# A two-layer kernel: convolution in half-length passes of 256 channels, and nine rows in the middle sample products

## The chip, the cores and the metric

The kernel runs on one core of a Trainium2 chip. The metric is device time in microseconds (us); lower is better. All arithmetic is fp32. The engines are TensorE (PE, matmuls, with its weight loads shown as PEld), VectorE (DVE), ScalarE (ACT), GpSimd (POOL) and SyncE (SP); SP, ACT and POOL also issue DMAs.

## What is computed

The input x has 32 images of 128 channels and 32 x 32 pixels (L = 1024). Layer 0 is a group norm, an encoder to 1024 channels, a causal convolution of 64 taps for each channel, a GELU, a gated linear unit, a layer norm and a decoder. Layer 1 is a group norm and a deformable convolution of 8 x 8 taps for each channel, whose sampling offsets are a depthwise 3 x 3 convolution of its input. Both are added to their inputs. Cut to what matters:

```python
# layer 0, on u = group_norm(x), (B, 128, L)
h = jnp.einsum('bdl,de->ble', u, W_enc) + b_enc
K = 2.0 * jnp.einsum('dn,dnl->dl', Cc * Bd, vand).real      # 64 taps a channel
z = jnp.swapaxes(h, 1, 2)
y = irfft(rfft(z, n=L + 64) * rfft(K, n=L + 64), n=L + 64)[..., :L] + D[:, None] * z
y = gelu(swapaxes(y, 1, 2))
g = y @ W_glu + b_glu
g = g[..., :1024] * sigmoid(g[..., 1024:])
out = layernorm(h + g) @ W_dec + b_dec
# layer 1, on v = group_norm(x1): for each of 64 taps
px = gx[None] + koff_t[0] + off_t[..., 0]
py = gy[None] + koff_t[1] + off_t[..., 1]
ix, iy = px * sx - 0.5, py * sy - 0.5                        # sx = sy = 32/31
acc = acc + bilinear(v, iy, ix) * w_t[None, :, None, None]   # four gathers, 0 outside
```

## The kernel before

`tile_two_layer_kernel` runs four parts in turn. `ssm_kernel_table` works out the 64 taps of each channel and writes them to DRAM as `kp_d`, a row of 320 for each channel, reversed and padded with zeros. `ssm_convolution` makes y, the convolved and GELUed channels, in DRAM as `y_d`. `main_block` does the rest of layer 0 and layer 1. `deformable_redo` compares the largest offset of every image with `BOUND_X` and `BOUND_Y` and, for images beyond it, runs a general gather path; otherwise it does nothing more.

**The convolution stage** is written in a fixed order (`manual_schedule`): for each of eight blocks of 128 channels, `encode` and then `convolve`. In `encode` every image is eight matmuls, each with 128 positions of u as weights and 128 columns of `W_enc` moving; four fill one PSUM tile, which VectorE adds the bias to and writes into the tile z (line 227). z is 128 positions on the partitions, and for each channel four position blocks of 32 images; two such tiles of 64 KB a partition hold the two halves of the length. In the first block `encode` also computes the group norm of every image and stores it as `u_d`; the other seven load u again, 512 KB an image, five buffers ahead (line 236).

`convolve` goes over the block in groups of eight channels (`CG`). The convolution of one 128-position block is a matmul (line 299) with z as weights and a Toeplitz tile moving: for each channel 128 partitions x 192 columns, where partition p holds the row of `kp_d` shifted by p. Two triangles of it are zeros, and they are loaded with the rest (line 281, 768 KB a group, three buffers). Of the 192 result columns 128 belong to the block itself and 64 run over into the next one. ScalarE copies these to SBUF (line 307), VectorE adds them to the next block's partitions in PSUM (line 311; `ORDER` places the blocks so that a 64- and a 32-partition add do it, and one more takes the overlap from the first half of the length to the second), and ScalarE then writes the GELU into `yo` (line 320). The GELU of one tile is emitted after the next tile's copies and adds. A group of eight channels is stored by eight DMAs that POOL issues (line 332), four for each of two `yo` tiles out of six buffers. PSUM has two tiles for the encode and three for the convolution.

**The main block** interleaves two streams by an estimate of their cost (`run_along`): `first_part` of image b + 2, 292 matmuls of 512 columns (gate products at line 757, value products at line 780, encoder and decoder at lines 796 and 685), and `second_part` of image b, the sample products. The first two images' `first_part` and the last two images' `second_part` have no partner of that kind.

A sample product turns bilinear sampling into matmuls (line 1091). The image, transposed, is the weights: windows of 8 columns by 16 rows of pixels, so 128 on the partitions. Moving is `ds`, the product of two hat functions (line 1048), with one column for each slot (pairs of tap column and output column, 8 to 16 of them together), tap row ky and output row. The 17 packs of slots sum to 256; ky comes in four pieces of two; and the 32 output rows are cut in three by `rows_of(piece)`, for the windows that begin at rows 0, 8 and 16. Before, the middle cut has eight rows and begins at 15, 13, 11 and 9. A moving operand is therefore made of short runs of consecutive elements, one run of that many rows for each slot and ky. VectorE multiplies the result with the tap weights (line 1094), and GpSimd adds the two ky (line 1111) and accumulates (line 1116). How far an offset may go before a sample leaves its window is `BOUND_Y`. An fp32 matmul appears in the trace as two passes, each a weight load and a matmul record.

Of the kernel before, what the change touches and what calls it, by code (L numbers as in the profile page):

```python
# [7 lines left out]
F32 = mybir.dt.float32  # L8
AF = mybir.ActivationFunctionType
# [3 lines left out]
DRAM = bass.MemoryType.DRAM  # L13

P = 128
B, C, H, W = 32, 128, 32, 32
L = H * W
D = 1024
KD = D // P
# [6 lines left out]
TW = 192  # L26

KP0 = TW - 1
KPW = 320
CG = 8  # L30
# [152 lines left out]
def ssm_convolution(nc, tc, const, ins, x, u_d, kp_d, y_d):  # L183
# [5 lines left out]

    ORDER = (0, 2, 1, 3)
    NB = NJ // 2
    RW = TW - P
    QC = 4
    with tc.tile_pool(name="cvt", bufs=3) as tp, tc.tile_pool(
        name="cvz", bufs=1
    ) as zp, tc.tile_pool(name="cv1", bufs=1) as one, tc.tile_pool(
        name="cvu", bufs=5
    ) as up, tc.tile_pool(name="cvy", bufs=6) as yp, tc.tile_pool(  # L200
        name="cvg", bufs=4
    ) as gp, tc.tile_pool(
        name="cv_psz", bufs=2, space=PSUM
    ) as psz, tc.tile_pool(name="cv_psy", bufs=3, space=PSUM) as psy:
        w_enc = one.tile([P, D], F32, tag="w_enc", name="w_enc")
        nc.sync.dma_start(w_enc, ins["W_enc"])
        b_enc = one.tile([P, D], F32, tag="b_enc", name="b_enc")
        nc.sync.dma_start(b_enc, ins["b_enc_row"].to_broadcast([P, D]))

        def encode(k):  # L210

            z = [
                pool.tile([P, P, NB, B], F32, tag=f"z{g}", name=f"z_{k}_{g}")
                for g, pool in enumerate((one, zp))
            ]
            bias = b_enc[:, k * P : (k + 1) * P]

            def image(b, u):
                for g in range(2):
                    ps = psz.tile([P, NB, P], F32, tag="ps", name=f"psz_{k}_{b}_{g}")  # L220
                    for j in range(NB):
                        lo = (NB * g + ORDER[j]) * P
                        nc.tensor.matmul(  # L223
                            ps[:, j, :], u[:, lo : lo + P], w_enc[:, k * P : (k + 1) * P],
                            start=True, stop=True,
                        )
                    nc.vector.tensor_add(  # L227
                        z[g][:, :, :, b].rearrange("p d j -> p j d"),
                        ps,
                        bias[:, None, :].to_broadcast([P, NB, P]),  # L230
                    )

            if k > 0:
                for b in range(B):
                    u = up.tile([P, L], F32, tag="u", name=f"u_{k}_{b}")
                    nc.sync.dma_start(u, u_d[b])
                    image(b, u)
                return z

# [7 lines left out]
            for t in range(B + 3):  # L247
# [4 lines left out]
                if t < B:  # L252
                    u = up.tile([P, L], F32, tag="u", name=f"u_{k}_{t}")
# [10 lines left out]
                step(t)  # L264
            return z

        def convolve(k, z):
            rows = [t.rearrange("p d j b -> p d (j b)") for t in z]
            waiting = []

            def finish():
                for work in waiting:
                    work()
                waiting.clear()

            for g in range(P // CG):
                d0 = k * P + g * CG
                toe = tp.tile([P, CG, TW], F32, tag="toe", name=f"toe_{d0}")
                table = kp_d[d0 : d0 + CG, 0:TW]

                nc.sync.dma_start(
                    toe,
                    bass.AP(
                        tensor=table.tensor,
                        offset=table.offset,
                        ap=[[1, P], [KPW, CG], [1, TW]],
                    ),
                )
                yo = [
                    yp.tile([P, CG, P], F32, tag="yo", name=f"yo_{d0}_{i}") for i in range(2)  # L290
                ]
                for q in range(CG // QC):
                    c0 = q * QC
                    last = None
                    for i in range(2):
                        ps = psy.tile([P, 2, 512], F32, tag="ps", name=f"psy_{d0}_{q}_{i}")
                        ps = ps[:, :, : 2 * TW].rearrange("p h (c n) -> p h c n", c=2)
                        for c in range(QC):
                            nc.tensor.matmul(  # L299
                                ps[:, c // 2, c % 2, :],  # L300
                                rows[i][:, g * CG + c0 + c, :],
                                toe[:, c0 + c, :],
                                start=True,
                                stop=True,
                            )
                        over = tp.tile([P, 2, 2, RW], F32, tag=f"t{i}", name=f"t_{d0}_{q}_{i}")
                        nc.scalar.copy(over, ps[:, :, :, :RW])  # L307

                        def carry(to, rows, src):
                            own = ps[to : to + rows, :, :, P:TW]  # L310
                            nc.vector.tensor_add(own, own, src)  # L311

                        carry(64, 64, over[0:64])
                        carry(32, 32, over[64:96])
                        if i > 0:
                            carry(0, 32, last[96:P])
                        finish()

                        def gelu(to=yo[i][:, c0 : c0 + QC, :], ps=ps):
                            nc.scalar.activation(  # L320
                                to.rearrange("p (h c) l -> p h c l", c=2),
                                ps[:, :, :, RW:TW][:, :, :, ::-1],
                                AF.Gelu_apprx_tanh,
                            )

                        waiting.append(gelu)
                        last = over

                def store(yo=yo, d0=d0):
                    for i in range(2):  # L330
                        for j in range(NB):
                            nc.gpsimd.dma_start(  # L332
                                y_d[d0 : d0 + CG, :, i * NB + ORDER[j], :].rearrange(
                                    "d b l -> b d l"
                                ),
                                yo[i][j * B : (j + 1) * B],
                            )

                waiting.append(store)
            finish()  # L340


        with tc.manual_schedule():
            for k in range(KD):
                convolve(k, encode(k))


def deformable_general(nc, tc, const, ins, x1_d, out, image):
# [139 lines left out]
KY2 = 2  # L488
# [10 lines left out]
    (24, (30, 31)), (24, (32, 33)), (24, (34, 35, 36, 37)),  # L499
)  # L500
YWINDOWS = (0, 8, 16)
BOUND_X, BOUND_Y = 2.45, 3.25
HSUB = NCOL // P


# [5 lines left out]

def rows_of(piece):

    a, b = 15 - KY2 * piece, 23 - KY2 * piece
    return (0, a), (a, b - a), (b, H - b)


def weight_slots():
# [27 lines left out]
def main_block(nc, tc, const, ins, x, u_d, y_d, x1_d, out, offmax):  # L546
# [21 lines left out]
    with ctx:  # L568
# [562 lines left out]
        def measure(columns):  # L1131
# [3 lines left out]
        SECOND = sum(  # L1135
            measure(slots_of(n) * KY2 * ny)
            for n in range(NP) for i in range(PIECES) for _, ny in rows_of(i)
        )

# [178 lines left out]
```

## Time and profile before

| what | us |
|---|---|
| median of three runs | 13584.75 (13580.38 to 13586.92) |
| the profiled execution | 13588.92 |
| its span, first to last instruction | 13587.2 |
| of it, before the last matmul of line 299 ends | 1448 |
| sample products (L1091), busy, 13056 records | 4701.1 |
| gate and value products (L757, L780), busy, 8192 records each | 3986.4 and 3975.7 |
| convolution matmuls (L299), busy, 4096 records | 704.7 |
| encode matmuls (L223), busy, 4096 records | 568.6 |
| bias adds of the encode (L227), busy, 512 records | 516.2 |
| issues of y stores on POOL (L332), busy, 1024 records | 590.1 |

Busy times of one engine may overlap each other in time: matmuls are pipelined and their ends are modelled, so the pace of a matmul is read from start to start. A share of the whole span says little here, since the convolution stage (the first tenth) and the main block (the rest) have different limits.

### The profile page before, as it was taken

The numbers are of one execution on the slowest core, as the hardware profiler recorded it, in microseconds if no ns is written. First come the engines' busy times: TensorE is split into PE (matmuls) and PEld (weight loads), VectorE is DVE, ScalarE is ACT, GpSimd is POOL, SyncE is SP. The second block draws the span as 40 slices with busy tenths as digits, with TensorE's granted clock in tenths as the row PEclk, the third lists the DMA queues.
The fourth block names the chain that finished last, engine by engine and source line by source line (L and its number), as shares of the span: only waits on it lengthen the run. The fifth ranks groups of instructions, "written<-read, shape, count | busy, mean of one in ns | idle before, by whom it ended". The sixth has DMA issues, their size and how long they took to land.

```text
span 13587.2 us, 133930 instructions
## 1 busy us (share of the span) xinstructions
PE 13106.8 (96%) x40482; PEld 7248.5 (53%) x40482; DVE 8781.8 (65%) x12685; ACT 3291.8 (24%) x4767; POOL 9080.3 (67%) x8868
## 2 busy tenths in 40 slices
PE   7999899999999999999999999999999999999975
PEld 7888545555555555555555555555555555555533
DVE  7787226666666666666666666666666666666677
ACT  4333222222211122222222211112222222221145
POOL 2444227777777777777777777777777777777778
PEclk9999999999999999999999999999999999999988
DMA  7888428888888888888889888888888888988876
GB/s 244 275 277 273 132 90 231 234 239 236 231 227 231 233 235 238 238 236 232 230 234 239 235 229 229 231 232 237 238 237 236 232 230 235 240 235 231 230 198 175
DMA packets 1715626, 3105.77 MB, mean 229 GB/s; under 512 B 308306, under 2 KB 1018322, under 8 KB 1713874
## 3 DMA queue, kind: packets, MB, share of 16 engines
q1 hardware_dynamic: 1502290, 2641.91, 73.2%
q10 hardware_dynamic: 163456, 320.92, 6.6%
q0 software_dynamic: 49152, 134.28, 2.9%
q8 instruction: 329, 5.39, 0.2%
q14 instruction: 399, 3.27, 0.1%
HBM read 2630.36 MB, written 466.06 MB: 228 GB/s over the span
## 4 chain that ended last, share of the span: by engine, by line
PE 81%; DMA 9%; DVE 4%; ACT 2%; POOL 2%; issue 1%; SPq 1%; ACTq 0%; DVEq 0%; POOLq 0%
PE gpv L780 24%; PE gpg L757 23%; PE dps L1091 23%; DMA ds<-dhat 4%; PE gph L796 3%; PE gpo L685 3%; PE psy L299 3%; PE psz L223 2%; DMA y_d<-yo 2%; DMA dhat<-dh 2%; DVE z L227 1%; DVE ds L1048 1%; DMA dhy<-dhat 1%; POOL y_d L332 1%; ACT ds L1040 0%
## 5 line engine op out<-in xcount | busy, mean ns | idle before, releaser
L1094 DVE TENSOR_TENSOR dp<-dps,k_weight_slots 128x256 f32<-128x256 f32 (+17 forms) x6528 | 3087.1, 483 | 3109.5 <-PE dps L1091 2914.8
L1091 PE MATMUL dps<-ds,dxw 128*128 128x256 f32 (+18 forms) x13056 | 4701.1, 447 | 223.5 <-DVE ds L1048 177.5
L1116 POOL TENSOR_TENSOR dacc<-dacc,dp 128x256 f32<-128x256 f32 (+3 forms) x4736 | 4417.4, 933 | 396.5 <-DVE dp L1111 26.6
L1091 PEld LDWEIGHTS dps<-ds,dxw 128*128 128x128 f32 x13056 | 2472.7, 192 | 3203.6 <-issue 2537.5
L757 PE MATMUL gpg<-gy,g_w_glu 128*128 128x512 f32 x8192 | 3986.4, 593 | 23.5 <-DMA gy<-y_d 15.7
L780 PE MATMUL gpv<-gy,g_w_glu 128*128 128x512 f32 x8192 | 3975.7, 592 | 0.0
L1111 POOL TENSOR_TENSOR dp<-dp 128x448 f32<-128x448 f32 (+2 forms) x2142 | 2675.1, 1249 | 1882.1 <-DVE dp L1094 1879.4
L1048 DVE TENSOR_TENSOR ds<-ds,dhy 128x1024 f32<-128x1024 f32 (+3 forms) x2176 | 3148.6, 1447 | 762.4 <-DMA ds<-dhat 647.9
L757 PEld LDWEIGHTS gpg<-gy,g_w_glu 128*128 128x128 f32 x8192 | 1546.9, 190 | 1235.8 <-issue 964.9
L780 PEld LDWEIGHTS gpv<-gy,g_w_glu 128*128 128x128 f32 x8192 | 1551.7, 190 | 1155.3 <-issue 913.8
L818 POOL TENSOR_TENSOR gs<-gs,gq 128x512 f32<-128x512 f32 x448 | 628.5, 1403 | 1341.3 <-ACT gq L817 1341.3
L817 ACT ACTIVATE gq<-gr 128x512 f32<-128x512 f32 x448 | 282.3, 630 | 4673.6 <-DVE gr L809 4611.2
L332 POOL DMA_DIRECT2D y_d<-yo x1024 | 590.1, 583 | 869.7 <-ACT yo L320 699.2
L764 ACT ACTIVATE gs<-gpg,k_b_glu 128x512 f32<-128x512 f32 x512 | 351.8, 687 | 2488.0 <-PE gpg L757 2377.6
L953 ACT ACTIVATE dh<-dr,k_minus 128x624 f32<-128x624 f32 x768 | 621.7, 809 | 642.5 <-DMA dhat<-dh 563.1
L299 PE MATMUL psy<-toe,z 128*128 128x192 f32 x4096 | 704.7, 333 | 45.2 <-ACT yo L320 43.8
L299 PEld LDWEIGHTS psy<-toe,z 128*128 128x128 f32 x4096 | 667.5, 192 | 81.6 <-ACT yo L320 74.5
L311 DVE TENSOR_TENSOR psy<-psy,t 32x256 f32<-32x256 f32 (+1 forms) x1280 | 553.7, 433 | 204.7 <-ACT t L307 162.6
L788 DVE SCALAR_TENSOR_TENSOR gs<-gpv,k_b_glu,gs 128x512 f32<-128x512 f32 x512 | 379.7, 742 | 437.3 <-PE gpv L780 437.2
L687 POOL TENSOR_TENSOR gs<-gs,gr 128x512 f32<-128x512 f32 x448 | 634.7, 1417 | 0.0
L954 ACT ACTIVATE dh<-dh,one 128x624 f32<-128x624 f32 x768 | 626.3, 815 | 25.0
L223 PE MATMUL psz<-w_enc,u 128*128 128x128 f32 x4096 | 568.6, 293 | 44.9 <-DVE z L227 32.3
(162 smaller groups left out, 6052.4 us busy)
## 6 DMA issues: line engine op xcount, KB each, us to landing
dhy<-dhat SPq DMA_DIRECT2D x1536, 512.0 KB
ds<-dhat SPq DMA_DIRECT2D x1440, 512.0 KB
dhat<-dh ACTq DMA_DIRECT2D x768, 312.0 KB
y_d<-yo POOLq DMA_DIRECT2D x1024, 128.0 KB, 5.4
gy<-y_d SPq DMA_DIRECT2D x512, 256.0 KB
u<-u_d SPq DMA_DIRECT2D x224, 512.0 KB
toe<-kp_d SPq DMA_DIRECT2D x128, 768.0 KB
dxw<-dvt_d SPq DMA_DIRECT2D x1248, 64.0 KB
```

Source lines behind the costliest of these rows:

```text
L223: nc.tensor.matmul(ps[:, j, :], u[:, lo : lo + P], w_enc[:, k * P : (k + 1) * P], start=True, stop=True,)
L299: nc.tensor.matmul(ps[:, c // 2, c % 2, :], rows[i][:, g * CG + c0 + c, :], toe[:, c0 + c, :], start=True, stop=True,)
L332: nc.gpsimd.dma_start(y_d[d0 : d0 + CG, :, i * NB + ORDER[j], :].rearrange("d b l -> b d l"), yo[i][j * B : (j + 1) * B],)
L687: nc.gpsimd.tensor_add(sums[0], sums[0], r)
L757: nc.tensor.matmul(gate, w_glu[:, k, D + m * P : D + m * P + P], ys[k], start=(k == 0), stop=(k == KD - 1),)
L780: nc.tensor.matmul(val, w_glu[:, k, m * P : m * P + P], ys[k], start=(k == 0), stop=(k == KD - 1),)
L818: nc.gpsimd.tensor_add(sums[1], sums[1], sq)
L1048: nc.vector.tensor_mul(s[:, :m], s[:, :m], hy[:, :m])
L1091: nc.tensor.matmul(ps, xw[:, j, :], s[:, :m, :, y0 : y0 + ny], start=True, stop=True)
L1094: nc.vector.tensor_mul(prod[:, :m, :, y0 : y0 + ny], ps, w[:, :, :, None].to_broadcast([P, m, KY2, ny]),)
L1111: adder.tensor_add(prod[:, :m, 0], prod[:, :m, 0], prod[:, :m, 1])
L1116: nc.gpsimd.tensor_add(to, to, prod[:, slot : slot + nj, 0])
```

## The change

It has two parts that do not touch each other.

In the convolution stage, a pass is now 256 channels (`ZC`) of half the length, so four blocks of channels times two halves. z is one tile of the same 128 KB a partition. An image is four encode matmuls of 256 moving columns instead of eight of 128, u is loaded by halves (256 KB), and except in the first pass every fourth PSUM tile is evacuated by a ScalarE copy and a GpSimd add of the bias in place of the VectorE add. The Toeplitz tiles become three fixed tiles that are zeroed once; for every group of every half two DMAs, one for each 64 partitions, load only the band of 128 columns that is not always zero. The overlap from the first half of the length to the second goes through DRAM (`edges`): POOL stores it for each group in the first half, SP loads it in the second. `yo` has five buffers instead of six, one tile a group.

In the main block the middle cut of `rows_of` has nine rows instead of eight, beginning at 14, 12, 10 and 9, the last cut has one row less or the first has, and `BOUND_Y` goes from 3.25 to 2.25.

```diff
     ORDER = (0, 2, 1, 3)
+    ZC = 256
+    NTOE = 3
...
-    ) as up, tc.tile_pool(name="cvy", bufs=6) as yp, tc.tile_pool(
+    ) as up, tc.tile_pool(name="cvy", bufs=5) as yp, tc.tile_pool(
...
+        toes = []
+        for i in range(NTOE):
+            toe = one.tile([P, CG, TW], F32, tag=f"toe{i}", name=f"toe{i}")
+            nc.gpsimd.memset(toe, 0.0)
+            toes.append(toe)
+
+        def encode(k, half):
+
+            z = one.tile([P, ZC, NB, B], F32, tag="z", name=f"z_{k}_{half}")
+            chans = slice(k * ZC, (k + 1) * ZC)
 
             def image(b, u):
-                for g in range(2):
-                    ps = psz.tile([P, NB, P], F32, tag="ps", name=f"psz_{k}_{b}_{g}")
-                    for j in range(NB):
-                        lo = (NB * g + ORDER[j]) * P
+                for g in range(NB // 2):
+                    ps = psz.tile([P, 2, ZC], F32, tag="ps", name=f"psz_{k}_{half}_{b}_{g}")
+                    for j in range(2):
+                        lo = ORDER[2 * g + j] * P
                         nc.tensor.matmul(
-                            ps[:, j, :], u[:, lo : lo + P], w_enc[:, k * P : (k + 1) * P],
+                            ps[:, j, :], u[:, lo : lo + P], w_enc[:, chans],
                             start=True, stop=True,
                         )
...
+                    if (k > 0 or half > 0) and (2 * b + g) % 4 == 3:
+                        nc.scalar.copy(to, ps)
+                        nc.gpsimd.tensor_add(to, to, bias)
+                    else:
+                        nc.vector.tensor_add(to, ps, bias)
...
-                    nc.sync.dma_start(u, u_d[b])
+                    u = up.tile([P, NB * P], F32, tag="u", name=f"u_{k}_{half}_{b}")
+                    nc.sync.dma_start(u, u_d[b, :, half * NB * P : (half + 1) * NB * P])
...
-                table = kp_d[d0 : d0 + CG, 0:TW]
-
-                nc.sync.dma_start(
-                    toe,
-                    bass.AP(
-                        tensor=table.tensor,
-                        offset=table.offset,
-                        ap=[[1, P], [KPW, CG], [1, TW]],
-                    ),
-                )
...
+                toe = toes[g % NTOE]
+
+                table = kp_d[d0 : d0 + CG, TW - P : TW]
+                for r in (0, 64):
+                    nc.sync.dma_start(
+                        toe[r : r + 64, :, 64 - r : 64 - r + P],
+                        bass.AP(
+                            tensor=table.tensor,
+                            offset=table.offset,
+                            ap=[[1, 64], [KPW, CG], [1, P]],
+                        ),
+                    )
+                if half > 0:
+                    edge = tp.tile([B, 2, 2, 2, RW], F32, tag="edge", name=f"edge_{d0}")
+                    nc.sync.dma_start(edge.rearrange("b q h c l -> b (q h c l)"), edges[g])
+                over = tp.tile([P, 2, 2, 2, RW], F32, tag="over", name=f"t_{d0}_{half}")
+                yo = yp.tile([P, CG, P], F32, tag="yo", name=f"yo_{d0}_{half}")
...
+                    if half > 0:
+                        carry(0, 32, edge[:, q])
...
+                    if half == 0:
+                        nc.gpsimd.dma_start(
+                            edges[g], over[96:P].rearrange("b q h c l -> b (q h c l)")
+                        )
...
-            for k in range(KD):
-                convolve(k, encode(k))
+            for k in range(D // ZC):
+                edges = dram.tile(
+                    [ZC // CG, B, CG * RW], F32, tag="edges", name=f"edges_{k}"
+                )
+                for half in range(2):
+                    convolve(k, half, encode(k, half), edges)
...
-BOUND_X, BOUND_Y = 2.45, 3.25
+BOUND_X, BOUND_Y = 2.45, 2.25
...
-    a, b = 15 - KY2 * piece, 23 - KY2 * piece
-    return (0, a), (a, b - a), (b, H - b)
+    a = (14, 12, 10, 9)[piece]
+    return (0, a), (a, 9), (a + 9, H - a - 9)
```

## The prediction

> **What bounds the kernel now.** I read the page first, then a table of busy time by stage, then the DMA queues and the timeline inside the stages that the change touches. The page:
>
> ```profile
> PE 13106.8 (96%) x40482; PEld 7248.5 (53%) x40482; DVE 8781.8 (65%) x12685; ACT 3291.8 (24%) x4767; POOL 9080.3 (67%) x8868
> ...
> DMA  7888428888888888888889888888888888988876
> ...
> L1091 PE MATMUL dps<-ds,dxw 128*128 128x256 f32 (+18 forms) x13056 | 4701.1, 447 | 223.5 <-DVE ds L1048 177.5
> ```
>
> The span has two parts. From 0 to 1448 us is the convolution stage: eight encodes (L223) each followed by a convolution (L299). From 1491 us on is the main block, where gate products (L757, L780) and sample products (L1091) are interleaved. TensorE is the bound of the main block, as the table by stage shows (columns: window, its length, then busy us and count of PE, PEld, DVE, ACT, POOL, then clock, DMA share, GB/s):
>
> ```profile
> 347.00:440.00 93.00, 88.20 (x514) 83.83 (x513) 68.55 (x158) 55.31 (x125) 64.06 (x112) 0.98 0.89 292
> 440.00:514.00 74.00, 68.61 (x513) 61.44 (x513) 65.48 (x68) 1.99 (x4) 9.64 (x17) 1.00 0.80 259
> ...
> 2500.00:6000.00 3500.00, 3478.78 (x9545) 1788.38 (x9544) 2259.11 (x3181) 746.90 (x988) 2524.72 (x2327) 1.00 0.87 235
> ```
>
> In the third row PE is busy 99.4% at full clock and nobody else is above 72%: a nanosecond taken from a matmul there comes off the end. The first two rows are one convolution and the next encode; by the first and last matmul of each line the eight pairs run 31 to 178 us (encode with the group norm), then convolutions of 91 to 95 us, mean 94, and seven encodes of about 74.3. The convolution looks PE-bound, but inside it the DMA engines are full:
>
> ```profile
> 367.00:377.00 10.00, 10.00 (x61) 9.50 (x60) 8.21 (x19) 6.81 (x16) 7.58 (x14) 1.00 0.99 316
> 377.00:387.00 10.00, 10.00 (x61) 9.47 (x60) 7.97 (x20) 6.41 (x16) 7.92 (x14) 1.00 1.00 322
> ...
> 417.00:427.00 10.00, 7.98 (x39) 7.69 (x38) 5.17 (x12) 3.87 (x10) 5.44 (x10) 0.83 0.98 333
> ```
>
> and near the end of it PE waits for a GELU that waits for a store to leave its buffer (timeline; the bracket is the idle time and its releaser):
>
> ```profile
> 434.52 0.60 ACT L320 ACTIVATE yo<-psy 128x512 f32<-128x512 f32 x1 [1.36 <-DMA y_d<-yo]
> ...
> 435.17 5.47 PE L299 MATMUL psy<-toe,z 128*128 128x192 f32 x32 [1.17 <-ACT yo L320]
> ```
>
> So the convolution stands at the point where DMA takes over from PE. The queues there price both kinds of packet: 367 to 407 us first (q1 is the Toeplitz loads, q0 the y stores), then 460 to 500 us, where q1 is the u loads alone:
>
> ```profile
> q1 hardware_dynamic: 7840, 5.93, 52.0%
> q0 software_dynamic: 2433, 6.66, 46.1%
> ```
> ```profile
> q1 hardware_dynamic: 2478, 9.00, 69.8%
> ```
>
> The share times 16 engines times 40 us: 333 engine-us over 7840 Toeplitz packets is 0.0424 us for 768 B; 295 for 6.66 MB of y is a full-rate 361 GB/s; 447 for 9.00 MB of u is 322 GB/s, so 0.203 us for 4 KB.
>
> [...]
>
> **The change, part by part.**
>
> Toeplitz loads. Before: 16 groups a pass, each 1024 packets of 768 B: 16384 x 0.0424 / 16 = 43.4 us of all engines in each convolution. After: 32 groups, two DMAs each, together 1024 packets of 512 B. The trace has no 512 B load; a line through the two prices (0.203 at 4096 B, 0.0424 at 768 B) gives an estimated 0.030. 32768 x 0.030 / 16 = 61.4 us. Bounds: bytes alone at 361 GB/s, 16.8 MB, 46.5 us[...]. I take 61.4[...].
>
> y stores. The same 1024 stores of 128 KB, 128 a convolution: 16.8 MB / 361 = 46.5 us, before and after.
>
> Overlap through DRAM. 128 stores and 128 loads of 64 KB are new: 2.1 MB in each convolution, 5.8 us. A store is also one more POOL issue in the first halves, at most the 0.583 us of L332: 5 a group, 2.9 us beside PE's 2.7, 93 us a convolution, so it binds only if DMA does not. The over tile (three buffers) is now read by a DMA queued behind y stores, so ScalarE's copy three groups later waits for it, and behind that copy its GELUs and PE.
>
> DMA in a convolution thus goes from 43.4 + 46.5 = 89.9 us to 61.4 + 46.5 + 5.8 = 113.7. What lies outside: three Toeplitz groups are loaded during the encode (-5.8), about three or four groups of y may lag into the next encode (-5), the first five u of the next encode come in (+4, 1.3 MB), and the engines idle until the first buffer is freed (some 3 us, against about 8 now: DMA share 0.28 at 347 to 357). 113.7 - 5.8 - 5 + 4 + 3 = 110 us. The same sum for before is 89.9 - 8.1 - 8.7 + 8.2 + 8 = 89 where 94 is measured: there PE's own 64 x 1.35 = 86 us is as long and the two hinder each other. From 94 to 110 is +16, times eight: +128 us. PE's work is unchanged: 64 tiles of four matmuls of 192 columns.
>
> u loads. 512 KB become 256 KB, minus 26 us of DMA in each encode, but these are not late: DMA stands at 0.7 there. Worth nothing by itself; it clears the y backlog sooner.
>
> Encode. 64 tiles before and after. Now two tiles take 2.29 us (fill 0.985, DVE 1.03, the two semaphores 0.28), the round trip of one PSUM buffer:
>
> ```profile
> 1001.32 1.97 PEld L223 LDWEIGHTS psz<-w_enc,u 128*128 128x128 f32 x16 [0.33 <-DVE z L227]
> 1002.51 2.05 DVE L227 TENSOR_TENSOR z<-psz,b_enc 128x512 f32<-128x512 f32 x2 [0.25 <-PE psz L223]
> ```
>
> With 256 columns the fill is four passes of 0.215 (half of the 0.430 that a 512-column pass takes start to start), 0.86. Every fourth tile goes to ACT (0.6) and POOL, but all of these fall on the odd buffer; the even one keeps DVE: 0.86 + 1.03 + 0.28 = 2.17 a pair, 69.4 us: minus 4. The last tile of a pass is an ACT and POOL one, and the first convolution matmul waits for it: 0.6 + a POOL add of about 2 us (1.4 at L818[...]) instead of 1.03: plus 2. At the worst the add takes the 4.9 us of L1122 for half its elements, still about the 4.3 that four tiles last. Net -2 x 7 = -14 us. The first encode keeps its 147 us: same norms, x loads and u stores.
>
> Nine rows. The weights and columns of the sample products stay, 65536 columns a pass and image; only their cut into three changes. But start to start, passes with eight rows cost more:
>
> ```profile
> 6004.37 0.54 PE L1091 MATMUL dps<-ds,dxw 128*128 128x208 f32 x2
> 6004.74 1.02 PE L757 MATMUL gpg<-gy,g_w_glu 128*128 128x512 f32 x2
> ...
> 6009.54 0.65 PE L1091 MATMUL dps<-ds,dxw 128*128 128x286 f32 x2
> 6010.02 1.88 PE L780 MATMUL gpv<-gy,g_w_glu 128*128 128x512 f32 x4
> ```
>
> 0.185 us for 208 columns (13 slots, 8 rows) is 0.89 ns each, 0.24 for 286 (11 rows) is 0.839, the rate of 512. Sorted so from 4000 to 5500 us, the excess over 0.8385 ns a column, per run of consecutive columns, is 0.59, 0.75, 0.68, 1.04 ns for the eight-row runs of the four pieces, 0.38 and 0.26 for nine, 0.27 and 0.15 for thirteen, 0.11 and 0.02 for eleven, 0 for fifteen; sum 4.23. [...] There are 1024 runs per cut and image (256 slots, two ky, two passes): 1.8 to 3.1 us an image, over the 30 images beside gate products 54 to 93. I take 65. DVE's multiplies have the same elements (0.415 us at 256, 0.452 at 288, 0.655 at 480: near a line).
>
> The tighter bound, 2.25 rows, matters only if an offset passes it, since then the general path runs for that image. The reference's offsets, worked out from its inputs, reach 2.096 in y and 2.378 in x (bound 2.45): it does not run.
>
> Sum on the span of 13587.2: +128 - 14 - 65 = +49, 13636. The profiled execution took 13588.9, 4 above the median of 13584.8; with that, 13632 to 13638 is one number; I say 13635.
>
> **Rivals.**
> One, faster: DMA copes. Packet times in a full queue contain waiting, so 512 B may cost bytes only; then 113.7 becomes 99, the wall 95, and the convolutions stay at PE's pace. -14 - 65 gives 13510. For it: 400 GB/s in single slices. Against: share 0.99 at 316 GB/s over tens of us, and 21% more bytes.
> Two, much slower:[...] One mechanism, the 64-partition loads[...]. Against: the y stores, from 32 partitions, run at 361 GB/s in the mix.
> Three, no change: packets at 285 GB/s as now (59 us) with a longer y lag, 104 a convolution, +80, against -79: 13586.
>
> **How the numbers follow.** Forecast 0.45, one 0.24, two 0.14, three 0.17. 0.2%, 27 us, is what a measurement tells from no change. Faster: case one, less its slower tail, plus some of three: 0.25. Same: most of three and the forecast's lower edge: 0.15. Slower 0.6. The forecast's own range is 13590 to 13700; with parts of one and two, 13505 to 13790.
>
> **What would show it.** Convolutions of about 110 us with a DMA share near 1 from start to end, PE waiting on GELU and that on y or overlap DMAs; Toeplitz packets near 0.030 us; encodes near 72; nine-row passes of 288 columns near 0.245 us and an image shorter by 2 us. Convolutions of 94 or less make it wrong towards faster, 130 towards slower; an image period unchanged removes the 65.

## The result and the profile after

| | before | after |
|---|---|---|
| median, us | 13582.7 (13580.4 to 13586.9) | 13771.5 (13765.2 to 13774.3) |
| span of the profiled execution | 13587.2 | 13763.4 |

The ratio is 1.0137 [1.0124, 1.015]: 189 us slower. 13635 was forecast, +49, in a range of 13505 to 13790. The direction was right and the size four times too small. The two profiled executions differ by 176 us, the medians by 189. The page of the kernel after answers to the lines shown of before (in groups: busy us, mean ns of one, idle time before and its releaser):

```profile
PE 13034.0 (95%) x38434; PEld 7096.5 (52%) x38434; DVE 8689.0 (63%) x12573; ACT 3408.9 (25%) x4879; POOL 9434.3 (69%) x9111
...
DMA  7877706888888888888888888888888888888876
...
L1106 PE MATMUL dps<-ds,dxw 128*128 128x288 f32 (+20 forms) x13056 | 4619.5, 440 | 243.7 <-DVE ds L1063 183.3
...
L309 PE MATMUL psy<-toe,z 128*128 128x192 f32 x4096 | 736.8, 336 | 189.1 <-DMA toe<-kp_d 97.9
```

The sample products (L1106, L1091 before) are busy 82 us less. The loss is at the other end: the convolution matmuls now stand idle before Toeplitz loads (97.9 of 189.1 us of idle time). By the first and last matmul of each line in the timeline, the span divides so (us):

| stage | predicted | before | after | difference |
|---|---|---|---|---|
| up to the first convolution matmul | 0 | 178.0 | 187.3 | +9 |
| eight convolutions | +128 | 748.8 | 905.2 | +156 |
| seven encodes with the gap behind each | -14 | 522 | 555 | +33 |
| everything after, mostly the main block | -65 | 12139 | 12117 | -22 |
| sum | +49 | 13587 | 13763 | +176 |

The table of busy time by stage (columns as before: window, length, PE, PEld, DVE, ACT, POOL, clock, DMA share, GB/s) shows the second convolution, the encode after it, and the main block:

```profile
380.00:490.00 110.00, 90.98 (x506) 83.08 (x507) 80.11 (x186) 57.13 (x124) 69.19 (x121) 0.98 0.99 300
490.00:568.00 78.00, 65.33 (x264) 44.35 (x262) 53.34 (x54) 18.34 (x21) 30.36 (x23) 1.00 0.46 141
2500.00:6000.00 3500.00, 3466.76 (x9581) 1792.16 (x9580) 2284.77 (x3200) 720.44 (x956) 2572.28 (x2355) 1.00 0.86 233
```

In the convolution PE is busy 83% and DMA 99%, where PE had 95% and DMA 89%: the bound has changed hands. In the encode PE, DVE and DMA all have room, so the order in which the engines wait for each other limits it. In the main block PE fell from 99.4 to 99.1% of the time: it has less to do and waits more.

The chain of waits inside the second convolution (start, length, what) names the load:

```profile
409.83 6.68 DMA toe<-kp_d
416.51 0.14 issue
416.65 2.85 PE psy L309 x16
419.50 0.02 issue
419.52 0.57 SPq L291
420.09 0.05 issue
420.14 8.21 DMA toe<-kp_d
```

A group's 16 matmuls free a tile, SP issues the load into it (0.57 us), it lands 6.3 to 8.5 us later in this stretch, and PE waits for it. The DMA queues from 400 to 460 us (packets, MB, share of 16 engines) give the prices:

```profile
q1 hardware_dynamic: 19092, 10.20, 60.1%
q0 software_dynamic: 3334, 9.13, 46.1%
```

0.601 x 16 x 60 us over 19092 packets is 0.0302 us for a Toeplitz packet of 512 B (overlap loads included), where 0.030 was estimated. 9.13 MB of y in 0.461 x 60 us is a full-rate 330 GB/s, down from 361.

The encode, in the timeline (the bracket is the idle time and its releaser; L229 fills, L236 and L237 are the new copy and add, L239 the VectorE add):

```profile
904.93 1.03 ACT L236 COPY z<-psz 128x512 f32<-128x512 f32 x1 [3.49 <-PE psz L229]
...
906.03 1.79 POOL L237 TENSOR_TENSOR z<-z,b_enc 128x512 f32<-128x512 f32 x1 [2.89 <-ACT z L236]
906.30 2.36 DVE L239 TENSOR_TENSOR z<-psz,b_enc 128x512 f32<-128x512 f32 x2 [1.22 <-PE psz L229]
...
911.26 1.91 DVE L239 TENSOR_TENSOR z<-psz,b_enc 128x512 f32<-128x512 f32 x2 [1.22 <-PE psz L229]
```

The ScalarE copy takes 1.03 us, about as long as a VectorE add (1.11 in the mean of 400). Beside the GpSimd add a pair of VectorE adds takes 2.36 us in one round and 1.91 in the next, and so it alternates: four tiles take 4.96 and 4.52 us, start to start. Both rounds have a GpSimd add beside them; why only one of them is slower stays open.

### The profile page after: what moved, and what is told of

Read it like the earlier page. It is cut to its first block, busy times and chain, and to the rows that moved or that the text cites. A ratio compares the mean times of both kernels' runs of the same rounds, so it can differ in the third digit from the quotient of the medians.

```text
span 13763.4 us, 131151 instructions
## 1 busy us (share of the span) xinstructions
PE 13034.0 (95%) x38434; PEld 7096.5 (52%) x38434; DVE 8689.0 (63%) x12573; ACT 3408.9 (25%) x4879; POOL 9434.3 (69%) x9111
## 3 DMA queue, kind: packets, MB, share of 16 engines
q10 hardware_dynamic: 163456, 320.92, 6.5%
## 4 chain that ended last, share of the span: by engine, by line
PE 79%; DMA 10%; DVE 4%; POOL 2%; issue 2%; ACT 1%; SPq 1%; ACTq 0%; DVEq 0%; POOLq 0%
PE gpg L772 24%; PE gpv L795 23%; PE dps L1106 22%; DMA ds<-dhat 4%; PE gph L811 3%; PE gpo L700 3%; DMA toe<-kp_d 2%; PE psz L229 2%; DVE z L239 2%; PE psy L309 2%; DMA y_d<-yo 1%; DVE ds L1063 1%; DMA dhy<-dhat 1%; POOL do L1137 1%; POOL dacc L1131 1%
## 5 line engine op out<-in xcount | busy, mean ns | idle before, releaser
L1109 DVE TENSOR_TENSOR dp<-dps,k_weight_slots 128x288 f32<-128x288 f32 (+14 forms) x6528 | 3094.8, 483 | 3208.5 <-PE dps L1106 3037.4
L1106 PE MATMUL dps<-ds,dxw 128*128 128x288 f32 (+20 forms) x13056 | 4619.5, 440 | 243.7 <-DVE ds L1063 183.3
L1131 POOL TENSOR_TENSOR dacc<-dacc,dp 128x256 f32<-128x256 f32 (+3 forms) x4736 | 4466.4, 943 | 396.0 <-DVE dp L1126 26.0
L1106 PEld LDWEIGHTS dps<-ds,dxw 128*128 128x128 f32 x13056 | 2471.5, 192 | 3223.1 <-issue 2585.4
L833 POOL TENSOR_TENSOR gs<-gs,gq 128x512 f32<-128x512 f32 x448 | 633.6, 1414 | 1285.0 <-ACT gq L832 1285.0
L309 PE MATMUL psy<-toe,z 128*128 128x192 f32 x4096 | 736.8, 336 | 189.1 <-DMA toe<-kp_d 97.9
L320 DVE TENSOR_TENSOR psy<-psy,t 64x256 f32<-64x256 f32 (+1 forms) x1024 | 446.2, 436 | 376.7 <-ACT t L316 351.8
L229 PE MATMUL psz<-w_enc,u 128*128 128x256 f32 x2048 | 537.2, 406 | 104.5 <-DVE z L239 83.1
```

Of the source, the lines that this page charges most:

```text
L229: nc.tensor.matmul(ps[:, j, :], u[:, lo : lo + P], w_enc[:, chans], start=True, stop=True,)
L309: nc.tensor.matmul(ps[:, c // 2, c % 2, :], rows[:, g * CG + c0 + c, :], toe[:, c0 + c, :], start=True, stop=True,)
L833: nc.gpsimd.tensor_add(sums[1], sums[1], sq)
L1106: nc.tensor.matmul(ps, xw[:, j, :], s[:, :m, :, y0 : y0 + ny], start=True, stop=True)
L1109: nc.vector.tensor_mul(prod[:, :m, :, y0 : y0 + ny], ps, w[:, :, :, None].to_broadcast([P, m, KY2, ny]),)
L1131: nc.gpsimd.tensor_add(to, to, prod[:, slot : slot + nj, 0])
```

## The experiments

Each edit was timed beside runs of the kernel before on the same chip, and its ratio, with a 95% interval, is against these. Differences in us are of medians and can lie some 8 us off the ratio. Those to the kernel after, and most of those between edits, compare runs on different chips, where the medians of before were 13580 to 13584.

**The two halves of the change, each alone.** `rows_only` is the kernel before with the nine rows; `conv_only` is the kernel after with the old rows.

```diff
# rows_only, on before
-BOUND_X, BOUND_Y = 2.45, 3.25
+BOUND_X, BOUND_Y = 2.45, 2.25
-    a, b = 15 - KY2 * piece, 23 - KY2 * piece
-    return (0, a), (a, b - a), (b, H - b)
+    a = (14, 12, 10, 9)[piece]
+    return (0, a), (a, 9), (a + 9, H - a - 9)
```

> The kernel before with the nine-row cut alone (rows_of and BOUND_Y as after), convolution untouched. Theory A (the trace of after: matmul pace of the sample products down 2.2 us an image, but the stretch in which the hat tables are written and read again is held by DMA, so the image period falls only from 368.15 to 367.5): 20 to 25 us less than before, about 13560. Theory B (PE alone sets the main block, and the small gain of after comes from something that the convolution change does to it): 65 to 75 us less, about 13512.

```diff
# conv_only, on after
-BOUND_X, BOUND_Y = 2.45, 2.25
+BOUND_X, BOUND_Y = 2.45, 3.25
-    a = (14, 12, 10, 9)[piece]
-    return (0, a), (a, 9), (a + 9, H - a - 9)
+    a, b = 15 - KY2 * piece, 23 - KY2 * piece
+    return (0, a), (a, b - a), (b, H - b)
```

> The kernel after with the eight-row cut and the bound of before, so the convolution change alone. If the two parts add up, as they share no time: before + 198 + 5, about 13790, 20 us above after. If the rows gained their 65 and something else in the main block lost 45, about 13835.

`rows_only` 13569.1, ratio 0.9989 [0.9981, 0.9997], -15 us. `conv_only` 13789.8, 1.0153 [1.0137, 1.0168], +206 us, 18 above the kernel after. The parts add up within the noise. The nine rows are worth 15 to 20 us, not 65, and everything else is the convolution stage.

**One load of 128 partitions for the same packets.** The tile takes 128 columns at one place for all partitions instead of the slanted band. Partitions 64 to 127 thereby get zeros of the table's padding in place of their columns 0 to 63, so part of their taps is missing; packets and bytes stay.

```diff
# one_load, on after
-                for r in (0, 64):
-                    nc.sync.dma_start(
-                        toe[r : r + 64, :, 64 - r : 64 - r + P],
+                nc.sync.dma_start(
+                    toe[:, :, 64 : 64 + P],
...
-                            ap=[[1, 64], [KPW, CG], [1, P]],
+                        ap=[[1, P], [KPW, CG], [1, P]],
```

> After, with one DMA to 128 partitions for each Toeplitz tile in place of two to 64: the same 1024 packets of 512 B, the same bytes; rows 64 to 127 get the columns of rows 0 to 63, so half of the convolution's products are of other taps. [...]packets get cheaper and the convolutions fall from 113 us towards 100 or less, 13660 or below. Packet theory (a 512 B packet costs 0.030 us wherever it lands): within 25 us of after, a few us less for the saved issue of 0.6 us on SP.

13742.8, 1.012 [1.0104, 1.0135]: 29 us under the kernel after, a little more than the packet theory allows and far less than the fall to 13660 or below that cheaper packets were to bring. The intervals of the two ratios overlap, but the traces show where the time goes: the convolutions in first halves of the length take 111 to 116 us, as in the kernel after, and those in second halves fall from 109 to 115 down to 105.5 to 108.2, 23 us in all. The queues in the same window as above, a second half:

```profile
q1 hardware_dynamic: 19840, 10.77, 62.0%
q0 software_dynamic: 3454, 9.43, 41.6%
```

The Toeplitz packet is unchanged at 0.0300 us, but y runs at 9.43 / (0.416 x 60), 378 GB/s instead of 330. In all the DMA engines move 338 GB/s with one load against 323 with two. Whether the 64 partitions of a load or the mere number of loads makes the difference, no run separates; why the first halves gain nothing stays open too.

**Deeper buffers.** Four Toeplitz tiles instead of three, paid for with one `u` and one `yo` buffer.

```diff
# ntoe4, on after
-    NTOE = 3
+    NTOE = 4
-        name="cvu", bufs=5
-    ) as up, tc.tile_pool(name="cvy", bufs=5) as yp, tc.tile_pool(
+        name="cvu", bufs=4
+    ) as up, tc.tile_pool(name="cvy", bufs=4) as yp, tc.tile_pool(
```

> After, with four Toeplitz tiles instead of three (u and yo buffers four instead of five, to make room). Latency theory (the cycle load 7.2 us, use 2.85, issue 0.6 over three buffers is what sets 3.55 us a group): four buffers give 2.7 us a group, convolutions of 88 to 95 us, about 13620. Throughput theory (the DMA engines are full, and a load takes 7 us because it queues): convolutions stay at 110 to 115 us and the load takes 10 us; within 30 us of after.

13765.4, 1.0135 [1.012, 1.0151], 6 us under the kernel after, which is within the noise. From 400 to 480 us the loads in the chain of waits now take 7.1 to 10.0 us instead of 6.3 to 8.5: more are in flight and each lasts longer, and the shares of the two queues add up to 110% from 400 to 460 us. The limit is throughput, not latency. The buffers of `yo` that were given up could hide a gain, but GELUs waited for y stores only 4.7 us in all.

**The overlap left out.** A zeroed tile is added in the second half, and nothing is stored or loaded, so the carry from the first half of the length to the second is missing.

```diff
# no_edges, on after
-                    edge = tp.tile([B, 2, 2, 2, RW], F32, tag="edge", name=f"edge_{d0}")
-                    nc.sync.dma_start(edge.rearrange("b q h c l -> b (q h c l)"), edges[g])
+                    edge = still
...
-                    if half == 0:
-                        nc.gpsimd.dma_start(
-                            edges[g], over[96:P].rearrange("b q h c l -> b (q h c l)")
-                        )
```

> After, without the overlap through DRAM: no store, no load, the first block of the second half adds zeros instead, so 64 of its columns lack the carry-over. DMA theory (the overlap is 2.1 MB a convolution of a full queue): 6 us less in each convolution, 113 to 107, about 13720. Wait theory (the store behind y stores holds the over tile and ScalarE behind it, in first halves only): first halves fall by 12 us or more, second halves by 3 to 6.

13733.7, 1.0112 [1.0096, 1.0127], -38 us against after. First halves lose 4.6 us each, second halves 3.0, mean 3.8. That is near the price of the bytes (5.8 predicted); single convolutions gain 0.9 to 7.1. A wait of ScalarE for its `over` tile would have shown as a gain of 12 or more in the first halves alone, and did not.

**Whole rows.** The kernel after with 768 B loads again, one DMA to 128 partitions for each group, in both halves. So it changes the size of the packets and the number of loads.

```diff
# full_toe, on after
-                table = kp_d[d0 : d0 + CG, TW - P : TW]
-                for r in (0, 64):
-                    nc.sync.dma_start(
-                        toe[r : r + 64, :, 64 - r : 64 - r + P],
+                table = kp_d[d0 : d0 + CG, 0:TW]
+                nc.sync.dma_start(
+                    toe,
...
-                            ap=[[1, 64], [KPW, CG], [1, P]],
+                        ap=[[1, P], [KPW, CG], [1, TW]],
```

> After, with the Toeplitz tiles loaded whole again in one DMA, 768 B packets with the zeros. Packet theory: 32768 packets at 0.0424 us over 16 engines are 86.8 us a convolution against 61.4, so 25 us more in each, 138, about 13970. If only bytes counted (316 to 340 GB/s): 8.4 MB more, 25 us, the same; if the loads were not the bound, no more than 30 us above after in total.

13851.8, 1.0195 [1.0179, 1.021], +80 us against after where +200 was expected. The convolutions take a mean of 123.9 us, 10.8 more than after and 13.8 more than `one_load` (110.1), which shares the single load. The queue, same window:

```profile
q1 hardware_dynamic: 16404, 12.85, 67.9%
```

0.679 x 16 x 60 / 16404 is 0.0397 us, near the 0.0424 of before. By the packet prices, 32768 x (0.0397 - 0.0302) / 16 = 19 us a convolution; 10.8 came, or 13.8 against `one_load`. If packet times in a full queue contain waiting for the other stream, differences of them overstate, which would fit; `ntoe4` speaks for it, where the same packets took 0.668 x 16 x 60 / 18808 = 0.0341 us with one more tile in flight.

**The encode without ScalarE and GpSimd.** The branch for every fourth tile is gone and VectorE adds all.

```diff
# enc_dve, on after
-                    if (k > 0 or half > 0) and (2 * b + g) % 4 == 3:
-                        nc.scalar.copy(to, ps)
-                        nc.gpsimd.tensor_add(to, to, bias)
-                    else:
-                        nc.vector.tensor_add(to, ps, bias)
+                    nc.vector.tensor_add(to, ps, bias)
```

> After, with every bias add of the encode on VectorE, none by ScalarE and GpSimd. Theory A (the ScalarE copy takes 1.03 us, not 0.6, so the odd PSUM buffer is freed no sooner, and the pair of tiles that meets the GpSimd add is 0.44 us longer): seven encodes go from 76.5 to 70 to 73 us and the 2.8 us before each convolution to 0.2, about 40 to 60 us less than after, 13715. Theory B (VectorE is the bound of the encode and the other path relieves it): encodes of 78 us or more, 10 us above after.

13729.3, 1.0107 [1.0092, 1.0123], -42 us against after, as expected in total. The encodes take 72.7 to 75.7 us, 74.0 in the mean, and the gap behind each is 1.15 us instead of 2.8, where 0.2 was expected. In the traces that is 29 us; another 13 came off the convolutions (a mean of 111.5 us), for which there is no explanation. The helpers made the encode slower than no helpers.

**Band loads without the split of the length.** The kernel before, passes of 128 channels as they were, with the three zeroed tiles, the two band loads and the nine rows.

```diff
# band_rows, on before (with the nine rows)
+        toes = []
+        for i in range(3):
+            toe = one.tile([P, CG, TW], F32, tag=f"toe{i}", name=f"toe{i}")
+            nc.gpsimd.memset(toe, 0.0)
+            toes.append(toe)
...
-                toe = tp.tile([P, CG, TW], F32, tag="toe", name=f"toe_{d0}")
-                table = kp_d[d0 : d0 + CG, 0:TW]
+                toe = toes[g % 3]
+                table = kp_d[d0 : d0 + CG, TW - P : TW]
...
```

> The kernel before with two pieces of the change alone: the band of 128 columns loaded by two DMAs into three tiles zeroed once, and the nine rows; passes, encode and overlap as before. Packet theory: 16384 packets at 0.030 us instead of 0.0424, 31 us of DMA a convolution instead of 43, so the queue is no longer full and the convolutions fall from 94 to PE's 87 to 90: 35 to 55 us less, and with 15 from the rows and 9 given back at the start, 13530 to 13550. If PE alone sets the convolution: 13570, as with the rows alone.

13527.4, 0.9954 [0.9941, 0.9968], 54 us faster than before (62 by the ratio). The table of busy time by stage, the same convolution as shown of before:

```profile
347.00:440.00 93.00, 90.53 (x556) 85.78 (x555) 74.31 (x163) 55.44 (x124) 73.38 (x128) 1.00 0.94 288
367.00:407.00 40.00, 40.00 (x238) 37.87 (x237) 32.15 (x75) 26.62 (x60) 32.37 (x57) 1.00 0.98 283
```

PE is busy without a break for 40 us, and the convolutions fall from 93.6 to 87.4 us, PE's own 86 and little more. The band alone saves 6 us a convolution. The kernel after loads each band twice, once for each half of the length: 16384 x 0.0302 / 16 = 31 us more of DMA, beside the 3.8 of the overlap. By this sum the second load is what makes 113 us of 87; no run loads the bands once with the length split.

**Where the nine rows' gain went.** Their matmuls did become faster: the timeline of PE in the kernel after has a nine-row pass of 288 columns and what follows it:

```profile
6421.11 0.65 PE L1106 MATMUL dps<-ds,dxw 128*128 128x288 f32 x2
6421.60 1.02 PE L772 MATMUL gpg<-gy,g_w_glu 128*128 128x512 f32 x2
```

0.49 us for two passes is 0.245 each, as predicted. The excess over 0.8385 ns a column, summed over the runs of the four pieces, fell from 4.23 to 1.79 ns; times 1024 that is 2.5 us an image. But the image period, from start to start of 29 images, fell by only 0.7. PE stalls took the rest, and they gather in one sixteenth of the image. There the chain of waits of the kernel after reads:

```profile
6416.05 7.99 DMA dhat<-dh
6424.10 4.86 DMA ds<-dhat
6430.63 1.44 PE dps L1106 x2
```

and the queue that SP issues from (timeline):

```profile
6415.60 0.55 SPq L1044 DMA_DIRECT2D dhy<-dhat  x1
6424.10 0.51 SPq L1044 DMA_DIRECT2D ds<-dhat  x1
```

SP, which issues all hat loads, stands for 8 us until a hat store that ScalarE issued (L970) has landed; the load behind it comes too late, VectorE cannot form the next `ds`, and PE idles 2.08 us. By the code, the hats stored then are those of the next image, which no load reads until `ready`. The waits of SP's queue in the kernel after (total us, times, longest):

```profile
SPq L1044 <- DMA dhat<-dh: 272.2, 100, 8.8
SPq L1077 <- DMA dhat<-dh: 257.8, 69, 8.3
```

L1077 loads windows of the image, which have nothing to do with hats. L1044 loads hats. Before had 470 us of these two waits as well (L1062 for windows, L1029 for hats):

```profile
SPq L1062 <- DMA dhat<-dh: 256.6, 54, 9.0
SPq L1029 <- DMA dhat<-dh: 213.6, 110, 7.7
```

Four kernels tested what makes them matter. First, bytes: the hat stores of all but the first two images were halved, and those images read what is missing from the hats of the first two, so their sampling weights are partly not their own.

```diff
# half_hats_8 on before, half_hats_9 the same on rows_only
+                    if k == 0 and b >= 2:
+                        st[f"h{a}"] = kept[b % 2, a]
...
+                    n = HSUB if b < 2 else HSUB // 2
-                        at(st[f"h{a}"], k * NCOL, [[HSUB, P], [1, HSUB]]), t
+                        at(st[f"h{a}"], k * NCOL, [[HSUB, P], [1, n]]), t[:, :n]
```

> The kernel before (eight rows), but from the third image on each hat table is stored by its first half alone and kept from two images earlier otherwise, so the sampling weights are partly those of another image; 3.7 MB of stores less an image, in the stretch where the DMA engines are full. If DMA holds PE up there (4.05 us of PE stalls an image in the trace of before, 3.2 of them in that stretch): 2.5 to 4 us less an image, 75 to 120 us below before. If not: within 20 us of before.

> The same with the nine-row cut. If the rows' gain of 2.2 to 2.5 us of PE pace an image is eaten by that full stretch: with the stretch relieved the gain comes through, 60 to 75 us below half_hats_8. If it is eaten by something else, or was never there: 15 to 25 us below half_hats_8, as between rows_only and before.

`half_hats_8` 13562.4, 0.9983 [0.9977, 0.999], -21 us where -75 to -120 was expected. `half_hats_9` 13612.8, 1.0021 [1.0012, 1.003], +29 us: the nine rows cost 50 us there. DMA is busy in that stretch (in before a share of 0.90 from 6240 to 6270 us, where PE idles 2.56 us), yet both miss, and the bytes of the stores fall as the main cause. In `half_hats_9` the waits for hat stores changed place: 281.6 us before hat loads and 256.3 before window loads in `rows_only` became 490.6 and 0.4:

```profile
SPq L1032 <- DMA dhat<-dh: 490.6, 125, 8.9
```

Then a third buffer for the hats that ScalarE writes, and the hat stores issued by GpSimd; both on `band_rows`.

```diff
# hat3, on band_rows
-        spool, hypool, hatpool = pool("mbs", SB), pool("mbh", HB), pool("mbq", 2)
+        spool, hypool, hatpool = pool("mbs", SB), pool("mbh", HB), pool("mbq", 3)
```
```diff
# hat_pool, on band_rows
-                    nc.scalar.dma_start(
+                    nc.gpsimd.dma_start(
                         at(st[f"h{a}"], k * NCOL, [[HSUB, P], [1, HSUB]]), t
                     )
```

> band_rows with three buffers for the hat tables instead of two. If ScalarE, waiting in order for the store of the hat before last, delays the sigmoids and so PE (about 18 us of such waits an image): stalls fall by 2 us an image or more, 13470 or less. If the stretch is full of DMA whatever ScalarE does: within 20 us of band_rows, 13527.

> band_rows with the hat tables stored from GpSimd's queue instead of ScalarE's. In the traces SP's next load waits for a hat store (some 510 us in the main block of before, 530 in after), and PE's stalls sit where that begins, in the ninth sixteenth of an image. [...]SP no longer waits for hat stores, the stalls of 6.5 us an image fall to 2 to 4, and the rows' gain comes through: 13430 to 13480. If the stretch is simply full of DMA: SP waits as long for other loads, within 20 us of 13527. GpSimd issues 24 stores more an image (14 us of its 100 idle ones) and waits for ScalarE in order; if that delays its adds and with them PE, slower than 13550.

`hat3` 13528.0, 0.9958 [0.9945, 0.9972], the same as `band_rows`: ScalarE's own wait for a buffer, which fell from 492 to 17 us in all, is not the cause. SP's wait before the window loads (L1068) fell to 55 us without effect, so these were not what PE missed; the wait before the hat loads (L1035) stayed:

```profile
SPq L1035 <- DMA dhat<-dh: 280.9, 120, 8.9
SPq L1068 <- DMA dhat<-dh: 55.3, 31, 2.6
```

`hat_pool` 13441.2, 0.9898 [0.9882, 0.9915], as expected: 139 us faster than before, 86 faster than `band_rows` (76 by the ratios), with the same bytes and matmuls. From 2500 to 12800 us no wait of SP for a hat store is left; its queue now waits mostly for the buffers it loads into:

```profile
SPq L1035 <- DVE dp L1100: 2517.9, 932, 6.3
```

Side by side, in us an image. The period is the mean of 29 images, the other columns are means of ten, so a row adds up only roughly. PE work is the sum of the paces of its matmuls; stalls are what their starts lie apart beyond it. Each trace is of one execution: that of `rows_only` is the slowest of its 13 (13587.1 against a median of 13569.1), that of `hat_pool` the fastest of its four (13430.6).

| kernel | period | PE work | stalls | of them in the ninth sixteenth |
|---|---|---|---|---|
| before | 368.15 | 364.6 | 3.8 | 1.6 |
| after | 367.45 | 362.2 | 5.2 | 4.2 |
| rows_only | 368.04 | 362.2 | 6.5 | 5.4 |
| half_hats_8 | 367.48 | 364.6 | 3.1 | 0.8 |
| half_hats_9 | 369.29 | 362.2 | 7.05 | 6.1 |
| band_rows | 367.90 | 362.2 | 6.5 | 5.6 |
| hat3 | 367.78 | 362.2 | 5.8 | 4.9 |
| hat_pool | 364.61 | 362.2 | 2.5 | 1.6 |

Whenever the nine rows took 2.4 us of work out, the stalls grew by 1.4 to 4 us, all in the ninth sixteenth; with the stores off ScalarE's queue the period falls by 3.5 us against before, more than the 2.4 of work. Over most of the main block SP's wait before hat loads goes the same way as the stalls: 208 and 214 us with eight rows, 269 to 288 with nine, 491 in `half_hats_9`, none in `hat_pool`. `hat_pool` is the fastest kernel of the study and faster than both kernels that were compared. Moving the stores was tried neither in the kernel after nor with eight rows, so how much of the 86 us belongs to the rows is not separated. Nor is it shown which property of the move does it, the other issuing engine, the other kind of queue (on the page of before the 1024 y stores of 128 KB that GpSimd issues are the 134.28 MB of q0 software_dynamic, and the hat stores are among the 320.92 MB of q10 hardware_dynamic) or the moment at which the stores leave; ScalarE's own wait for its buffers is not it, since that grew to 806 us.

## Why the prediction was right and wrong

**The total: inside the range in part by luck.** The forecast's own range was 13590 to 13700. 13771 lies beyond it, and within 13505 to 13790 only through what rival two added, whose price was the author's estimate, shown by no trace, and did not come. All four terms missed to the same side: the encode by 47 us, the rows by 43, the convolutions by 28, the start by 9.

**The convolution becomes a DMA bound: right, but by another wait.** The packet price (0.030, measured 0.0302) and the DMA share came as said, and 113 us where 110 was said. The wait did not. "PE waiting on GELU and that on y or overlap DMAs" carried over what the kernel before showed, where GELUs stood idle 51.6 us for y stores in 34 waits. In the kernel after that is 3.5 us in 20 waits, and PE waits for the Toeplitz loads themselves. There is luck in the 110, too: the terms for what lies outside the convolution (-5.8, -5, +4, +3) were not measured afterwards, and the same sum gave 89 for the kernel before, where 93.6 was measured. A term that was mis-sized is the y stores, costed at 361 GB/s "before and after": at the measured 330 they are 16.8 MB / 330 = 50.9 us instead of 46.5, +4.4 a convolution. The overlap was 3.8 instead of 5.8. Together that would be +2.4 of the missing 3.2. `one_load` ties the slower y to the two 64-partition loads in the second halves. So rival two, which blamed the 64-partition loads, pointed at the right place at a small part of its price: one load for two takes 29 us off in all. Rival one, that DMA copes at PE's pace, is excluded by 113 us at a share of 0.99, and rival three by its 104 us a convolution.

**The encode at -14: wrong, +33 came.** Two terms failed. The first is "0.86 + 1.03 + 0.28 = 2.17 a pair, 69.4 us: minus 4". `enc_dve`, with VectorE alone, takes 2.26 a pair against 2.29 before, because the fill is 0.97 and not 0.86 (medians, start to start; before 0.995): the first pass after the wait for the buffer takes 0.32 us and only the others 0.216. The first pass of before had the same extra, 0.21 instead of 0.11, inside the 0.985 that was read. The wider columns saved next to nothing. With the helpers every other round costs 0.44 more, where VectorE's pair takes 2.36 instead of 1.91 beside the GpSimd add. The sum priced each engine as if the others stood still. 16 rounds of four tiles at half of 0.44 are 3.5 us an encode; the means of the encodes differ by 2.5 (76.5 and 74.0). The second is "instead of 1.03: plus 2" for the last tile. Before, the first convolution matmul needed only the first of two z tiles and followed the encode within 0.2 us; with one z tile it waits for the last evacuation, 1.15 us by VectorE and 2.8 by the helpers, so plus 2.65. Encodes of 76.5 instead of 74.5 and this gap are the +33. The prices of the helpers were off as well, in opposite directions: the copy 1.03 for 0.6, the GpSimd add 1.68 (median) for 2. The copy writes z with a step of 512 B and the GELU that gave the 0.6 does not, which may be the reason; no run separates it. The 2 was the author's estimate; measured, the add that reads z takes 1.19 times the 1.41 of an add of that size in the main block (L833).

**"The first encode keeps its 147 us": wrong by 9 us.** Its first matmul starts at 51.7 us instead of 31. In the timeline POOL's memset of the Toeplitz tiles waits 44 us for the last store of the taps table and the load of `W_enc` leaves at 47.2. `band_rows` has the same three memsets, which run at 3 us there, and its first encode matmul starts at 31. So it is not the 4 us of the memset, but that it and the load of `W_enc` wait for the store. That the new tiles lie where the taps' SBUF was is the likely reason, and was not tested.

**The nine rows: right in pace, wrong in what it is worth.** 2.5 us an image came against the 2.2 behind the 65. The lower end of the range for it, 1.8, takes nine-row runs at 0.32 ns, the mean of the 0.38 and 0.26 read from the trace; the upper end, 3.1, was the author's estimate and was not shown. The step that failed is "a nanosecond taken from a matmul there comes off the end". PE busy 99.4% hid stalls that are not slack but a chain of their own: SP's loads queued behind stores issued elsewhere. When PE ran faster, the stalls grew and gave most of the time back. -22 us came; cutting the chain, on `band_rows`, shortened the image by another 3.29, 99 us over 30 images, of the 106 by which the two profiled executions differ; the medians show 86.

## What to carry to other kernels

Splitting a pass reloads whatever does not depend on the split: count those packets at the stage that is nearest to its DMA limit (here 31 us more of DMA in a convolution of 87), and load less before splitting. A PE that is 99.4% busy can still stall, here 3.8 us of the 368 of an image; before a gain is booked at full value, look at what ends each stall and whether that chain follows PE or runs at its own pace. And when a queue of loads waits for stores that its data do not need, try early to issue those stores from another engine (here 76 to 86 us).

## What the runs showed that was not expected

- A queue of SP waited for stores of ScalarE that its loads do not read, some 500 us in all, and issuing these stores from GpSimd was worth 76 to 86 us at equal bytes. What ties these loads to these stores was not shown.
- A ScalarE copy of 512 elements a partition from PSUM costs 1.03 us when written with a step of 512 B, and the GELU of the convolution 0.60 us for as many elements, written without such a step. Whether the step makes the difference was not tested.
- Nine-row runs do not all cost the same: those that begin at rows 9 and 12 cost about 0.26 and 0.27 ns over the pace of 512 columns, those that begin at 14 and 10 only 0.06 to 0.08 (medians). What separates them was not shown.
